# One sample of a residual matmul gathered by GpSimd, without the rows of eight partitions

## The chip, the cores and the metric

The kernel runs on one core of a Trainium2 chip. The metric is the time of one execution on the device in microseconds (us), the median of several runs. The engines of the core are TensorE (PE, matrix products), VectorE (DVE), ScalarE (ACT), GpSimd (POOL) and SyncE (SP). Sixteen DMA engines move data between the large memory (HBM) and the on-chip memory (SBUF, 128 partitions); transfers are issued on queues that belong to an engine.

## The reference

```
x: (128, 128, 1024) f32      # samples b, channels c, times t
subjects: (128,) int32       # one of 8 per sample
weights: (8, 128, 128) f32   # c x d per subject

w = weights[subjects]
out = x + einsum('bct,bcd->bdt', x, w)
```

For each of the 128 samples a 128x128 matrix is chosen by the sample's subject; it is multiplied with the sample (128x1024), and the sample itself is added. 67 MB are read and 67 MB written.

## The kernel before

The samples go in 32 tiles (index `i`) of four samples each, a sample in the tile being `q` from 0 to 3. A tile is worked in two halves of two samples; the halves, here called pairs, have the running number `j` from 0 to 63. Tile `i` lies in buffer `i % 12` of `xs`, with the channels on the 128 partitions, so twelve tiles (24 MB) can be on the chip at once. The order of the work is written out by hand, with semaphores between the engines; no scheduler moves it.

Loads (line 121). ACT issues one transfer of 512 KB for each sample, in order. The source is cut so that four consecutive rows (`ROWS`), 16 KB, are one piece, and the four rows land in four neighbouring partitions. From tile 12 on, ACT first waits until the store of the tile that had the buffer before has landed (line 167). Each buffer has two semaphores `s_pair`, one for each half; every transfer adds 16 (`DMA`) to its half's.

Weights. All eight matrices lie in `w_all` (one transfer of 512 KB, line 161). For every sample GpSimd copies the matrix that the sample's subject names into one of four buffers (line 196); it reads the subjects from `index`, which VectorE prepares at the start (lines 153 to 157). The copy of a pair's first sample waits for the pair's loads and for the add of the pair before (`s_added`), so GpSimd's stream of copies is what releases each pair:

```
nc.gpsimd.wait_ge(s_added, j - P_SLOTS + 1)
copy = nc.gpsimd.tensor_copy(ws[b % W_SLOTS], w_all[:, bass.ds(subject[b % R], 1), :])
copy.wait_op(*loaded(i, q0), "sem-ge")
```

Products and sums. TensorE waits for the pair's copies and makes four products of 128x128 by 128x512 (line 206; a float32 product shows as two matmuls in the profile). VectorE adds the product to the samples, in place, one operation for each pair (line 217).

Stores (line 130). SP stores a whole tile (2 MB) after its second pair, and single halves or samples for the first and the last tile. At the end ACT waits for all stores (line 229).

At the start three matmuls on zeros run on TensorE (line 146). `emptied` and `loaded` compute the values of `s_pair` that mean that a buffer is free or filled.

Of the kernel before, what the change touches and what calls it, by code (L numbers as in the profile page):

```python
# [26 lines left out]
I32 = mybir.dt.int32  # L27
ALU = mybir.AluOpType


G = 2
H = 2
# [3 lines left out]
SLOTS = 12  # L36
# [5 lines left out]
DMA = 16  # L42

IDLE = 3

ROWS = 4
QUEUES = {mybir.EngineType.SP: "qSPDynamicHW", mybir.EngineType.Activation: "qActDynamicHW"}


def transfer(nc, engine, out, in_):  # L50

    later, nc._always_lower_symbolic_ap = nc._always_lower_symbolic_ap, False
    ins, outs = engine.lower_ap_dma(in_), engine.lower_ap_dma(out)
    nc._always_lower_symbolic_ap = later
    return engine.add_instruction(  # L57
        mybir.InstDMACopy(
            name=nc.get_next_instruction_name(),
            engine=engine.engine,  # L60
            ins=ins,
            outs=outs,
            mode="Copy",
            cce_op=ALU.bypass,
            queue=QUEUES[engine.engine],
        )
    )


@with_exitstack  # L70
def kernel(
    ctx: ExitStack,
    tc: tile.TileContext,
    x: bass.AP,
    subjects: bass.AP,
    weights: bass.AP,
    out: bass.AP,
):
    nc = tc.nc
    B, C, T = x.shape  # L80
    S, _, D = weights.shape
    NT = B // (G * H)

    def sbuf(name, *shape, dtype=F32):
        return ctx.enter_context(nc.sbuf_tensor(name, list(shape), dtype)).ap()

    given, near, wrap, index = (
        sbuf(name, 1, B, dtype=I32) for name in ("given", "near", "wrap", "index")
    )
    w_all = sbuf("w_all", C, S, D)  # L90
    ws = [sbuf(f"w{i}", C, 1, D) for i in range(W_SLOTS)]
    zeros = sbuf("zeros", C, N)
    xs = [sbuf(f"x{i}", C, H * G, T) for i in range(SLOTS)]
    ps = [
        ctx.enter_context(nc.psum_tensor(f"ps{i}", [D, G, T], F32)).ap() for i in range(P_SLOTS)
    ]

    s_given = tc.alloc_semaphore("s_given")
    s_wall = tc.alloc_semaphore("s_wall")
    s_index = tc.alloc_semaphore("s_index")  # L100
    s_zeros = tc.alloc_semaphore("s_zeros")
    s_copied = tc.alloc_semaphore("s_copied")
    s_product = tc.alloc_semaphore("s_product")
    s_added = tc.alloc_semaphore("s_added")

    s_pair = [[tc.alloc_semaphore(f"s_pair{i}_{h}") for h in range(H)] for i in range(SLOTS)]


    s_first = tc.alloc_semaphore("s_first")

    def emptied(i, h):

        turns = i // SLOTS
        return (DMA * G + (DMA if h == H - 1 else 0)) * turns

    def loaded(i, q):

        h = q // G
        return s_pair[i % SLOTS][h], emptied(i, h) + DMA * G

    def load(engine, i, q):
        k, h = i % SLOTS, q // G
        transfer(
            nc,
            engine,
            xs[k][:, q, :],
            x[i * H * G + q].rearrange("(a r) t -> a (r t)", r=ROWS),
        ).then_inc(s_pair[k][h], DMA)

    def store(i, q0, q1):  # L130
        k, b = i % SLOTS, i * H * G
        transfer(
            nc,
            nc.sync,
            out[b + q0 : b + q1].rearrange("g d t -> d g t"),
            xs[k][:, q0:q1, :].rearrange("d (o g) t -> d o (g t)", g=min(G, q1 - q0)),
        ).then_inc(s_first if i == 0 and q1 == G else s_pair[k][(q1 - 1) // G], DMA)

    with tc.tile_critical():  # L139

        nc.sync.dma_start(given, subjects.rearrange("(o b) -> o b", o=1)).then_inc(s_given, DMA)

        nc.vector.memset(zeros, 0.0).then_inc(s_zeros, 1)  # L143
        nc.tensor.wait_ge(s_zeros, 1)
        for _ in range(IDLE):
            nc.tensor.matmul(  # L146
                ps[P_SLOTS - 1][:, G - 1, :N], zeros[:, :D], zeros, start=True, stop=True
            )

        nc.vector.wait_ge(s_given, DMA)
        nc.vector.tensor_scalar(near, given, -S, S - 1, ALU.max, ALU.min).then_inc(s_index, 1)  # L153
        nc.vector.wait_ge(s_index, 1)
        nc.vector.tensor_scalar(wrap, near, 0, S, ALU.is_lt, ALU.mult).then_inc(s_index, 1)  # L155
        nc.vector.wait_ge(s_index, 2)
        nc.vector.tensor_tensor(index, near, wrap, ALU.add).then_inc(s_index, 1)  # L157
        nc.gpsimd.wait_ge(s_index, 3)


        nc.scalar.dma_start(w_all, weights.rearrange("s c d -> c s d")).then_inc(s_wall, DMA)  # L161
        for i in range(NT):
            k = i % SLOTS
            if i == SLOTS:
                nc.scalar.wait_ge(s_first, DMA)
            if i >= SLOTS:
                nc.scalar.wait_ge(s_pair[k][H - 1], emptied(i, H - 1))
            for q in range(H * G):
                load(nc.scalar, i, q)


        for j in range(NT * H):
            i, q0, q1 = j // H, j % H * G, (j % H + 1) * G
            k = i % SLOTS
            p = ps[j % P_SLOTS]

            ahead = j < P_SLOTS
            if ahead:  # L180
                nc.tensor.wait_ge(*loaded(i, q0))
            for q in range(q0, q1):
                b = i * H * G + q
                if b % R == 0:
                    _, subject = nc.values_load_multi_w_load_instructions(
                        index[0:1, b : b + R],
                        engines=[mybir.EngineType.Pool],
                        min_val=0,
                        max_val=S - 1,
                        skip_runtime_bounds_check_because="the index is clamped on the chip above",  # L190
                    )
                if b == 0:
                    nc.gpsimd.wait_ge(s_wall, DMA)
                if not ahead and q == q0:
                    nc.gpsimd.wait_ge(s_added, j - P_SLOTS + 1)
                copy = nc.gpsimd.tensor_copy(  # L196
                    ws[b % W_SLOTS], w_all[:, bass.ds(subject[b % R], 1), :]
                )
                if not ahead and q == q0:
                    copy.wait_op(*loaded(i, q0), "sem-ge")  # L200
            copy.then_inc(s_copied, 1)

            nc.tensor.wait_ge(s_copied, j + 1)
            for q in range(q0, q1):
                for t in range(0, T, N):
                    mm = nc.tensor.matmul(  # L206
                        p[:, q % G, t : t + N],
                        ws[(i * H * G + q) % W_SLOTS][:, 0, :],
                        xs[k][:, q, t : t + N],
                        start=True,  # L210
                        stop=True,
                    )
            mm.then_inc(s_product, 1)

            mine = xs[k][:, q0:q1, :]
            nc.vector.wait_ge(s_product, j + 1)
            nc.vector.tensor_tensor(  # L217
                mine, p, mine, ALU.add
            ).then_inc(s_added, 1)

            if i == 0 or q1 == H * G or i == NT - 1:
                nc.sync.wait_ge(s_added, j + 1)
                store(i, q0 if i in (0, NT - 1) else 0, q1 - (b == B - 1))

    with tc.tile_critical() as waits:
        for i in range(NT - SLOTS, NT):
            nc.scalar.wait_ge(s_pair[i % SLOTS][H - 1], emptied(i + SLOTS, H - 1))
        nc.scalar.wait_ge(s_pair[(NT - 1) % SLOTS][0], emptied(NT - 1 + SLOTS, 0) + DMA)  # L230
    last = nc.sync.dma_start(out[B - 1], xs[(NT - 1) % SLOTS][:, H * G - 1, :])

    tc.add_manual_dep(
        last.ins,
        waits.name,
        mybir.DependencyInfo(mybir.DependencyClass.NoSync, mybir.DependencyReason.SCHED_ONLY),
        reason="the end of the program waits for it",
    )
# [27 lines left out]
```

## Time and profile before

| | |
|---|---|
| median of 3 runs | 325.92 us (325.64 to 326.22) |
| the profiled execution | 326.15 us, span of its instructions 324.4 us |
| TensorE busy (matmul) | 240.2 us, 74% |
| VectorE busy | 147.9 us, 46% |
| GpSimd busy | 34.3 us, 11% |
| moved by DMA | 134.85 MB, mean 416 GB/s |

The span is cut into 40 slices of 8.1 us. A digit is the busy share in a slice in tenths, 9 being 90% or more. GpSimd's copies are 296 ns each, 128 of them; its idle time before them is 237.2 us, of which 207.2 us ended with the landing of a load.

### The profile page before, as it was taken

How to read it: one execution, taken by the hardware profiler on the slowest of the kernel's cores; microseconds unless marked ns; L12 is line 12 of the kernel's file. 1: busy time of each engine (PE TensorE's matmuls, PEld its weight loads, DVE VectorE, ACT ScalarE, POOL GpSimd, SP SyncE). 2: the span in 40 equal slices, each digit the busy share in tenths (PEclk: the TensorE clock that was granted, in tenths of full speed). 3: DMA queues.
4: the chain of work that ended last, by engine and by line, in shares of the span. 5: the costliest groups of instructions: out<-in, count | busy, mean ns of one | idle time of the engine just before them, and what ended most of it. 6: DMA issues, size and time to landing. Idle time of an engine off the chain costs nothing.

```text
span 324.4 us, 1608 instructions
## 1 busy us (share of the span) xinstructions
PE 240.2 (74%) x518; PEld 94.5 (29%) x518; DVE 147.9 (46%) x68; POOL 34.3 (11%) x132
## 2 busy tenths in 40 slices
PE   7999987888888888888988888888888768000000
PEld 2444432333333333333333333333333323000000
DVE  1475754555555555555555555554554553200000
POOL 1011110111111111111011111111111010000000
PEclk9999999999999999999999999999999999855555
DMA  7999999999999999999999999999999999999995
GB/s 263 402 418 426 426 421 425 425 425 423 428 425 422 427 418 427 427 424 424 428 423 421 423 427 426 419 429 426 423 426 427 417 435 417 425 427 424 429 426 243
DMA packets 16074, 134.85 MB, mean 416 GB/s; under 512 B 2625, under 2 KB 3650, under 8 KB 3906
## 3 DMA queue, kind: packets, MB, share of 16 engines
q10 hardware_dynamic: 7184, 67.64, 49.8%
q1 hardware_dynamic: 8882, 67.11, 49.3%
q8 instruction: 4, 0.07, 0.1%
q14 instruction: 4, 0.03, 0.0%
HBM read 67.63 MB, written 67.11 MB: 415 GB/s over the span
## 4 chain that ended last, share of the span: by engine, by line
PE 41%; DVE 20%; issue 18%; POOL 4%; DMA 2%; POOLq 1%; ACTq 0%; SPq 0%
PE ps L206 41%; DVE x L217 20%; POOL w L196 4%; DMA x<-in_x_dram 2%; POOLq L196 1%; ACTq L57 0%; ACTq L161 0%; ACTq L262 0%; SPq L139 0%
## 5 line engine op out<-in xcount | busy, mean ns | idle before, releaser
L206 PE MATMUL ps<-x,w 128*128 128x512 f32 x512 | 234.7, 604 | 33.6 <-POOL w L196 32.9
L217 DVE TENSOR_TENSOR x<-ps,x 128x2048 f32<-128x2048 f32 x64 | 146.7, 2292 | 128.1 <-PE ps L206 128.1
L206 PEld LDWEIGHTS ps<-x,w 128*128 128x128 f32 x512 | 92.6, 189 | 176.5 <-issue 92.3
L196 POOL COPY w<-w_all 128x128 f32 x128 | 34.1, 296 | 237.2 <-DMA x<-in_x_dram 207.2
L146 PE MATMUL ps<-zeros 128*128 128x512 f32 x6 | 5.5, 1088 | 1.7 <-DVE zeros L143 1.7
L146 PEld LDWEIGHTS ps<-zeros 128*128 128x128 f32 x6 | 1.8, 328 | 3.7 <-issue 2.1
L143 DVE MEMSET zeros<- 128x512 f32 x1 | 0.5, 485 | 1.1 <-SPq L139 1.1
L153 DVE TENSOR_SCALAR near<-given 1x128 int32<-1x128 int32 x1 | 0.2, 216 | 0.6 <-DMA given<-in_itok_B_dram 0.6
L157 DVE CUSTOM_DVE_ANT_0 index<-near,wrap 1x256 uint16<-1x256 uint16 x1 | 0.3, 278 | 0.0
L155 DVE TENSOR_SCALAR wrap<-near 1x128 int32<-1x128 int32 x1 | 0.2, 215 | 0.0
L253 POOL MEMSET const-float32-0.0<- 128x1 f32 x1 | 0.1, 99 | 0.2 <-issue 0.2
L253 POOL MEMSET const-bfloat16-1.0<- 128x1 bf16 x1 | 0.1, 102 | 0.0
L253 POOL MEMSET const-uint8-127<- 128x1 uint8 x1 | 0.1, 102 | 0.0
L253 POOL MEMSET const-float32-1.0<- 128x1 f32 x1 | 0.1, 99 | 0.0
## 6 DMA issues: line engine op xcount, KB each, us to landing
x<-in_x_dram ACTq DMA_DIRECT2D x128, 512.0 KB, 32.2
out_dram<-x SPq DMA_DIRECT2D x30, 2048.0 KB, 46.9
out_dram<-x SPq DMA_DIRECT2D x3, 1024.0 KB, 13.8
out_dram<-x SPq DMA_DIRECT2D x2, 512.0 KB, 21.0
w_all<-in_L_cond_weights_dram ACTq DMA_DIRECT2D x1, 512.0 KB, 4.3
given<-in_itok_B_dram SPq DMA_DIRECT2D x1, 0.5 KB
```

Source lines behind the costliest of these rows:

```text
L143: nc.vector.memset(zeros, 0.0).then_inc(s_zeros, 1)
L146: nc.tensor.matmul(ps[P_SLOTS - 1][:, G - 1, :N], zeros[:, :D], zeros, start=True, stop=True)
L153: nc.vector.tensor_scalar(near, given, -S, S - 1, ALU.max, ALU.min).then_inc(s_index, 1)
L155: nc.vector.tensor_scalar(wrap, near, 0, S, ALU.is_lt, ALU.mult).then_inc(s_index, 1)
L157: nc.vector.tensor_tensor(index, near, wrap, ALU.add).then_inc(s_index, 1)
L196: copy = nc.gpsimd.tensor_copy(ws[b % W_SLOTS], w_all[:, bass.ds(subject[b % R], 1), :])
L206: mm = nc.tensor.matmul(p[:, q % G, t : t + N], ws[(i * H * G + q) % W_SLOTS][:, 0, :], xs[k][:, q, t : t + N], start=True, stop=True,)
L217: nc.vector.tensor_tensor(mine, p, mine, ALU.add).then_inc(s_added, 1)
L253: nc = _bacc.Bacc("TRN2", target_bir_lowering=False, num_devices=1)
```

## The change

One sample, number 3 of tile 11 (the 48th load, sample 47), no longer comes by ACT's load. GpSimd issues one indirect DMA for it, right behind the copies of pair 19: each partition has an index of the row in HBM that belongs to it, and the row is 4 KB. An index beyond the end of `x` means that nothing is moved for that partition; this is set for partitions 16-19 and 48-51. Their eight rows come in two transfers of four rows each on ACT's queue, at the place where the load stood. The gather waits for both (`s_spared`) and for the index (`s_rows`); pair 23's second copy waits for the gather (`s_gathered`). The counts of the buffer's semaphore are lowered by the one transfer that no longer adds to it.

The index is made at the start: GpSimd counts the rows up (iota), and three small VectorE operations add the number of all rows (`B * C`) where the row's number, cut to the bits 0x5C, is 16.

```
+SPARE = (11, 3, 19)
+SPARED = (16, 48)
+SPARED_BITS = 0x5C
...
+    def load_spared(engine, i, q):
+        for p, landed in zip(SPARED, s_spared):
+            transfer(nc, engine, xs[i % SLOTS][p : p + 4, q, :], x[i * H * G + q, p : p + 4, :]).then_inc(
+                landed, DMA
+            )
+
+    def gather(i, q):
+        nc.gpsimd.wait_ge(s_rows, 4)
+        for landed in s_spared:
+            nc.gpsimd.wait_ge(landed, DMA)
+        nc.gpsimd.indirect_dma_start(
+            xs[i % SLOTS][:, q, :],
+            None,
+            x.rearrange("b c t -> (b c) t"),
+            bass.IndirectOffsetOnAxis(ap=rows, axis=0),
+            bounds_check=B * C - 1,
+            oob_is_err=False,
+        ).then_inc(s_gathered, DMA)
...
+        nc.gpsimd.iota(rows, [[0, 1]], base=(SPARE[0] * H * G + SPARE[1]) * C, channel_multiplier=1).then_inc(
+            s_rows, 1
+        )
+        nc.vector.wait_ge(s_rows, 1)
+        nc.vector.tensor_scalar(mark, rows, SPARED_BITS, None, ALU.bitwise_and).then_inc(s_rows, 1)
+        nc.vector.wait_ge(s_rows, 2)
+        nc.vector.tensor_scalar(mark, mark, SPARED[0], B * C, ALU.is_equal, ALU.mult).then_inc(s_rows, 1)
+        nc.vector.wait_ge(s_rows, 3)
+        nc.vector.tensor_tensor(rows, rows, mark, ALU.add).then_inc(s_rows, 1)
...
-                load(nc.scalar, i, q)
+                (load_spared if (i, q) == SPARE[:2] else load)(nc.scalar, i, q)
...
+                if (i, q) == SPARE[:2]:
+                    nc.gpsimd.wait_ge(s_gathered, DMA)
...
             copy.then_inc(s_copied, 1)
+            if j == SPARE[2]:
+                gather(*SPARE[:2])
```

## The prediction

> **What bounds the kernel now.** I read the two rows of slices first, then the DMA queues, then who waits for whom, and at last the end of the span cut into short stretches.
>
> ```profile
> DVE  1475754555555555555555555554554553200000
> POOL 1011110111111111111011111111111010000000
> DMA  7999999999999999999999999999999999999995
> GB/s 263 402 418 426 426 421 425 425 425 423 428 425 422 427 418 427 427 424 424 428 423 421 423 427 426 419 429 426 423 426 427 417 435 417 425 427 424 429 426 243
> ...
> q10 hardware_dynamic: 7184, 67.64, 49.8%
> q1 hardware_dynamic: 8882, 67.11, 49.3%
> q8 instruction: 4, 0.07, 0.1%
> ...
> x<-in_x_dram ACTq DMA_DIRECT2D x128, 512.0 KB, 32.2
> out_dram<-x SPq DMA_DIRECT2D x30, 2048.0 KB, 46.9
> ```
>
> The 16 DMA engines are full from the second slice to the last but one, at 417 to 435 GB/s. The load queue (q10) and the store queue (q1) share them, 49.8 and 49.3%. No other engine is near that. A store waits 46.9 us from issue to landing, so the stores stand in a long queue; a load waits 32.2 us. So work on the compute engines is late or early without cost as long as neither queue runs dry, and the time is what the slowest DMA engine has to carry.
>
> The next rows are GpSimd's copies in order of time, from the one of pair j = 19 (a pair is two samples) to that of j = 23.
>
> ```profile
> 82.04 0.53 POOL L196 COPY w<-w_all 128x128 f32 x2 [3.46 <-DMA x<-in_x_dram]
> 86.35 0.53 POOL L196 COPY w<-w_all 128x128 f32 x2 [3.77 <-DMA x<-in_x_dram]
> ...
> 98.99 0.53 POOL L196 COPY w<-w_all 128x128 f32 x2 [3.78 <-DMA x<-in_x_dram]
> ```
>
> Each copy has waited for its own pair of samples: the compute runs right behind the loads, one pair in (98.99 - 82.04) / 4 = 4.24 us. Sample 47, the one that the change treats, lands just before 98.99.
>
> Last, the end of the span in short stretches; the last two columns are the mean busy share of the 16 DMA engines and GB/s.
>
> ```profile
> 319.00:320.00 1.00, 0.00 (x0) 0.00 (x0) 0.00 (x0) 0.00 (x0) 0.50 1.02 418
> 320.00:320.40 0.40, 0.00 (x0) 0.00 (x0) 0.00 (x0) 0.00 (x0) 0.50 0.85 348
> 320.40:320.80 0.40, 0.00 (x0) 0.00 (x0) 0.00 (x0) 0.00 (x0) 0.50 0.68 277
> 320.80:321.20 0.40, 0.00 (x0) 0.00 (x0) 0.00 (x0) 0.00 (x0) 0.50 0.38 154
> 321.20:321.60 0.40, 0.00 (x0) 0.00 (x0) 0.00 (x0) 0.00 (x0) 0.50 0.32 133
> 321.60:322.00 0.40, 0.00 (x0) 0.00 (x0) 0.00 (x0) 0.00 (x0) 0.50 0.20 82
> 322.00:322.40 0.40, 0.00 (x0) 0.00 (x0) 0.00 (x0) 0.00 (x0) 0.50 0.10 41
> 322.40:322.90 0.50, 0.00 (x0) 0.00 (x0) 0.00 (x0) 0.00 (x0) 0.50 0.06 25
> 322.90:324.30 1.40, 0.00 (x0) 0.00 (x0) 0.00 (x0) 0.00 (x0) 0.50 0.00 0
> ```
>
> The engines do not end together. 0.06 of 16 engines is one engine: from 322.4 to 322.9 a single one still works, and the share of 0.10 in the stretch before says that the second ended at about 322.25. The trace's records have the last engine's final packet end at 322.95. So the last engine leads the second by 0.7 us and the mean engine by some 1.7, and the program waits for it. It is the only place where a transfer of this size can change the time. The late engines are probably those that carried a 16 KB packet of q8 (program code): four such packets took 0.97 to 1.10 us each in the trace's records, against 0.616 us for a 16 KB packet of a load.
>
> **The base.** The profiled execution took 326.15 us: a span of 324.4 and 1.75 around it. The median shown is 325.92, 0.23 less; I take differences from the profile and apply them to 325.92.
>
> **Part 1, sample 47 without eight partitions.** The load that is dropped is 32 packets of 16 KB (four rows of 4 KB each), two for each engine: 2 x 0.616 = 1.23 us of every engine. The gather brings the sample back in rows of 4 KB, except 16-19 and 48-51: these are just two of the 32 packets, which is what one engine carried. If they are one engine's two, that engine is rid of 1.23 us. The Trainium skill, page "DMA: Bandwidth & Descriptors", section "The descriptor swizzle", puts partitions 16-19 and 48-51 on the same DMA engine; no view of this profile names an engine. What is cut would then be more than the lead of 0.7, so the gain would be the lead and no more.
>
> **Part 2, the gather's own cost on the other 15 engines.** No row of before has a gather. Nearest below: the 4 KB packets of the last stores took 0.159 us each, so eight rows are 1.27 us instead of 1.23, +0.04. Farthest above: the 512-byte pieces of w_all, 512 KB that its 16 engines moved from 2.04 to about 4.8 us, 2.7 us each, so up to +1.5 if a gathered row went in small pieces. A gain below the first is excluded, since the bytes are the same. I take +0.04, because the rows have the size of the store's packets, and keep +1.5.
>
> **Part 3, the eight spared rows.** Two transfers of four rows in place of one load on ACT: one more issue, at 0.48 us (the shortest of the load issues) to 4.3 (the longest); ACT's loads land 32 us after their issue, so this is covered by their queue. On the DMA engines eight rows of 0.159 us. Spread over eight engines this is 0.16 each, over four 0.32, on one 1.27. The one tiny transfer of before (the index list) shows that a small transfer does not use all engines: it is one packet. I take 0.32 on four engines. The same page, section "Why a DMA increments its semaphore by 16 and not by 1", has a transfer of four partitions on four engines, the lowest-numbered; by that the sum would be the same 0.32.
>
> **Part 4, the stall on GpSimd.** The gather stands behind copy 19 and waits for the spared rows. They are last in tile 11's loads: behind sample 46, some 2.1 us before 98.99, so about 97. Until then GpSimd stands still, from 82.6 on. Behind it in its stream are the copies of pairs 20 to 23; TensorE, VectorE and the stores wait for those. Issuing the gather takes GpSimd between 0.48 and 4.3 us (the bounds of ACT's load issue). Copy 20 runs at 97.5 to 101.4 instead of 86.35, 11 to 15 us late, and TensorE is idle for about as long; if its clock falls, the first pair runs like the opening matmuls on zeros (1.06 us each, against 0.43 us from start to start later), +3.4 us. So pair 20 is up to 18.5 us late. What hides it is the store queue. Tile 10's store, due at 97.3, would be issued at about 109 to 116. Tile 9's store, issued at 88.7, lands about 51 us later (the median of the stretch from 60 to 120), at 139.8; only then, or from 137.5 on the first engine, does an engine need tile 10's. The margin is 21 us. After the stall a pair takes 3.43 us (the spacing of the adds at 15.03 and 18.47) against 4.24 of the loads, so the delay is made up in 18.5 / 0.81 = 23 pairs at most, while the store queue stays filled. The loads of tile 12 and later wait for stores that landed in the order and time of before. Pair 23 waits for the gather. If that landed as late as a load does, 32 us after its issue, it would be there at 133 at the latest; tile 11's store would be issued at about 140, and is needed when tile 10's ends, about 151. Cost: nothing. Without the queue of stores it would cost the 11 to 18 us.
>
> **Part 5, the index.** One iota on GpSimd (0.10 us, a memset of 128x1, to 0.30, a copy) and three small VectorE operations (0.22 + 0.22 + 0.28 = 0.7 us by their neighbours) are done before 5.4 us, when the first copy gets its weights, and VectorE is idle until 11.6. Even some us more would only move the first stores, while the loads fill the engines. Cost: nothing.
>
> **Sum.** If the relieved engine is the last: the end moves to the second, -0.70; the gather +0.04; -0.66. If the second is one of the four that take spared rows (about one chance in four), -0.34. I take -0.6: 325.3. That the cut fits the last engine is a choice and not a reading, since no view numbers the engines.
>
> **The rivals.**
> (a) Another engine is last, or the kept-out rows still burden theirs, so the last engine gets the gather's +0.04, 325.9 to 326.0. For it: nothing in the trace ties partitions 16-19 to the lone engine. Against it: if lateness follows from program code, it is the same engine in each run, and one engine's weight is the one thing that this change alters. The page's table in "Rules for kernel authors" says that spreading transfers over the three issuing engines brings no bandwidth. By that the time would be 325.9 as well; that total is not what part 1 is about.
> (b) Slower: the last engine is one of those that take spared rows, or the gather goes in small pieces. The first costs 0.04 + 0.32 = 0.36 (326.3), with all eight rows on it 0.04 + 1.27 = 1.3 (327.2); the second makes the second engine end 1.5 later, so 1.5 - 0.7 = +0.8 (326.7). It decides from 0.65 up: four rows on the last engine, or 1.4 us more for the gather. For it: a transfer of few rows sits on few engines. Against it: the 4 KB packets of the stores run at the rate of the big ones.
> (c) The stall is not hidden: the store queue would have to run dry, which needs pair 20 to be 40 us late (115 + 25 = 140). Nothing points there; then some us more, 328 to 335.
>
> **How the numbers follow.** The forecast 0.45, (a) 0.27, (b) 0.20, (c) 0.03, and 0.05 for more than the lead (the order of the engines' ends may differ without the profile; up to 1.2 us, 324.7). About 0.2%, 0.65 us, is what a measurement of this kernel can tell from no change. The forecast's -0.66 lies on that bound, so I give nearly 6 in 10 of it to faster: 0.27 + 0.05 = 0.32. Of (b) most is over the bound, with (c) 0.19 slower. The rest, 0.49, is within. The forecast's own range is 325.0 to 325.6; to hold 8 in 10 it takes in (a) and most of (b): 324.9 to 326.7.
>
> **What would show it.** Right: in the last stretches the share falls to zero at about 322.3, with the first lone stretch gone; a third hardware or software queue of about 0.49 MB; GpSimd silent from 82.6 to about 98 with the DMA row at 9 throughout; adds 3.4 us apart after it until about 190. Wrong: the lone engine still there at 322.9 or later (a); a longer tail, or a gather queue whose share is well over 0.4% of the engines (b); a dent in the DMA row after 137 (c).

## The result and the profile after

The changed kernel takes 327.14 us (326.78 to 327.42, six runs); the kernel before took 325.84 beside it. The ratio is 1.0035, with a 95% interval from 1.0025 to 1.0045: slower by 1.3 us, where the forecast was 325.3 and the range ended at 326.7. The profiled execution took 327.42 us, with a span of 325.6.

The page of the changed kernel, first the rows of slices, then the DMA queues and the row of the gather:

```profile
PE   6999987888606999999999898888889598000000
DMA  7999999999999999999999999999999999999996
GB/s 260 411 406 423 430 415 419 429 419 421 425 429 420 422 420 420 429 414 423 428 421 420 426 424 416 425 424 424 423 420 422 429 421 421 429 424 429 425 429 263
...
q10 hardware_dynamic: 7152, 67.15, 49.5%
q1 hardware_dynamic: 8882, 67.11, 49.4%
q0 software_dynamic: 144, 0.49, 0.4%
...
L154 POOL DMA_INDIRECT x<-in_x_dram,rows x1 | 1.2, 1168 | 15.6 <-issue 15.6
...
x<-in_x_dram,rows POOLq DMA_INDIRECT x1, 12.6
```

The stall is there (TensorE's slice of 0), and the DMA row stays at 9 through it. The gather has the forecast's 0.49 MB and 0.4% of the engines: in the records 120 packets of 4 KB and 24 of 4 bytes. (The run with all rows, below, has 128 and 16; so each kept-out row still leaves a packet of 4 bytes.) GpSimd's instructions in order of time show the stall and how it is made up:

```profile
82.71 0.53 POOL L240 COPY w<-w_all 128x128 f32 x2 [3.50 <-DMA x<-in_x_dram]
98.80 1.17 POOL L154 DMA_INDIRECT x<-in_x_dram,rows  x1 [15.56 <-issue]
99.98 0.99 POOL L240 COPY w<-w_all 128x128 f32 x4
109.73 0.53 POOL L240 COPY w<-w_all 128x128 f32 x2 [8.76 <-DVE x L263]
113.17 0.53 POOL L240 COPY w<-w_all 128x128 f32 x2 [2.91 <-DVE x L263]
...
168.10 0.53 POOL L240 COPY w<-w_all 128x128 f32 x2 [2.90 <-DVE x L263]
171.84 0.53 POOL L240 COPY w<-w_all 128x128 f32 x2 [3.21 <-DMA x<-in_x_dram]
```

From 109.73 the copies come 3.43 us apart and wait for VectorE; at 171.84 they wait for loads again. Whether the stall costs anything is tested below.

Then the end of the span, in stretches (the last two columns are the share of the DMA engines and GB/s):

```profile
321.60:322.00 0.40, 0.00 (x0) 0.00 (x0) 0.00 (x0) 0.00 (x0) 0.50 0.78 318
322.00:322.40 0.40, 0.00 (x0) 0.00 (x0) 0.00 (x0) 0.00 (x0) 0.50 0.63 256
322.40:322.90 0.50, 0.00 (x0) 0.00 (x0) 0.00 (x0) 0.00 (x0) 0.50 0.42 172
322.90:323.30 0.40, 0.00 (x0) 0.00 (x0) 0.00 (x0) 0.00 (x0) 0.50 0.43 174
323.30:324.00 0.70, 0.00 (x0) 0.00 (x0) 0.00 (x0) 0.00 (x0) 0.50 0.17 70
324.00:324.60 0.60, 0.00 (x0) 0.00 (x0) 0.00 (x0) 0.00 (x0) 0.50 0.02 7
```

All engines end later: seven of 16 (0.43) still work at 323, where before a single one was left at 322.4. Chained packet by packet, the trace's records give 16 ends; their mean went from 321.1 to 322.7 us. (The 16 increments of the last store's semaphore, 0.4 us behind, went from 321.52 to 323.13.) So it is not one engine that got more; something cost the engines 1.6 us on average.

Where it went is seen when the span is cut by what the queues do: from 40 to 240 us loads and stores alternate, from 280 to 315 only stores are left. Before, then after:

```profile
40.00:240.00 200.00, 174.96 (x380) 68.11 (x379) 108.65 (x48) 25.09 (x94) 1.00 1.01 425
280.00:315.00 35.00, 0.00 (x0) 0.00 (x0) 0.00 (x0) 0.00 (x0) 0.51 1.01 426
```

```profile
40.00:240.00 200.00, 171.75 (x377) 70.16 (x377) 107.72 (x48) 26.04 (x95) 0.96 1.01 422
280.00:315.00 35.00, 0.00 (x0) 0.00 (x0) 0.00 (x0) 0.00 (x0) 0.51 1.01 427
```

Engines fully busy in both, but 422 GB/s instead of 425 while the queues alternate, and no loss with stores alone. In the records of that stretch a store's 8 KB packet took 314.8 ns on average instead of 312.1, a load's 16 KB packet 619.35 instead of 616.5. The loss shows from about 28 us on, 9 us behind the first store and 70 us ahead of the gather. Each engine moves 268 of the first and 190 of the second in 200 us: 268 x 2.7 + 190 x 2.84 ns = 1.26 us. As an estimate that is 1.5 us over the 242 us (28 to 270) in which the loss shows.

The compute engines have no part in it. During the stall none of them does anything, and the loss is the same: from 90 to 98.8 us the packets took 314.7 and 620.3 ns.

```profile
90.00:98.80 8.80, 0.00 (x0) 0.00 (x0) 0.00 (x0) 0.00 (x0) 0.50 1.00 419
```

### The profile page after: what moved, and what is told of

Read it like the earlier page. It is cut to its first block, busy times and chain, and to the rows that moved or that the text cites. A ratio compares the mean times of both kernels' runs of the same rounds, so it can differ in the third digit from the quotient of the medians.

```text
span 325.6 us, 1618 instructions
## 1 busy us (share of the span) xinstructions
PE 239.2 (73%) x518; PEld 97.9 (30%) x518; DVE 148.2 (46%) x71; POOL 35.3 (11%) x134
## 4 chain that ended last, share of the span: by engine, by line
PE 37%; ACTq 20%; DMA 9%; DVE 8%; issue 8%; POOL 2%; POOLq 0%; SPq 0%
PE ps L252 37%; ACTq L63 20%; DMA x<-in_x_dram 9%; DVE x L263 8%; POOL w L240 2%; POOLq L240 0%; ACTq L203 0%; POOL x L154 0%; POOLq L153 0%; POOLq L154 0%; ACTq L308 0%; SPq L172 0%
## 5 line engine op out<-in xcount | busy, mean ns | idle before, releaser
L252 PEld LDWEIGHTS ps<-x,w 128*128 128x128 f32 x512 | 96.0, 193 | 173.8 <-issue 96.2
L154 POOL DMA_INDIRECT x<-in_x_dram,rows x1 | 1.2, 1168 | 15.6 <-issue 15.6
## 6 DMA issues: line engine op xcount, KB each, us to landing
x<-in_x_dram,rows POOLq DMA_INDIRECT x1, 12.6
```

Source lines behind the costliest of these rows:

```text
L154: nc.gpsimd.indirect_dma_start(xs[i % SLOTS][:, q, :], None, x.rearrange("b c t -> (b c) t"), bass.IndirectOffsetOnAxis(ap=rows, axis=0), ...
L252: mm = nc.tensor.matmul(p[:, q % G, t : t + N], ws[(i * H * G + q) % W_SLOTS][:, 0, :], xs[k][:, q, t : t + N], start=True, stop=True,)
```

## The experiments

What of the change works before the gather is issued? Two things were left. Theory A: the two index tiles (`rows`, `mark`) are allocated ahead of the weights and the samples. They take 32 bytes each in every partition, so all that lies behind them moves: the sample buffers begin at byte 26816 of a partition instead of 26752 (by the order and sizes of the tiles; no trace shows an address). Theory Q: the program now has a third queue, GpSimd's, and the engines lose time on it. The kernels of one group ran on one chip beside the kernel before (medians 325.97, 325.89 and 325.96 in the three groups). The packet times below are means of the records from 40 to 240 us.

**The shift alone.** The kernel before with an unused tile:

```
+    pad = sbuf("pad", C, 16)          # 64 bytes a partition
     w_all = sbuf("w_all", C, S, D)
```

> The kernel before with nothing but an unused tile of 64 bytes for each partition ahead of w_all, so that the sample buffers begin at byte 26816 of a partition instead of 26752, as in the changed kernel. In the changed kernel the packets of both queues take longer from the first store on, long before the gather: 622.5 against 619.3 ns for 16 KB of a load and 313.3 against 311.5 ns for 8 KB of a store, some 1.6 us for each DMA engine. Theory A (the shift of the buffers by 64 bytes does it): 325.84 + 1.6, about 327.4, with packets of 622 and 313 ns. Theory Q (the third queue, GpSimd's, does it): 325.8 as before, 619 and 311 ns.

Measured: 327.52 us, ratio 1.0049 (1.0037 to 1.0062); packets of 314.7 and 619.5 ns (over the whole run 313.2 and 621.4, the 313 and 622 of theory A). No gather, no third queue, and the whole loss. Its two stretches:

```profile
40.00:240.00 200.00, 173.89 (x377) 67.60 (x376) 107.81 (x48) 24.88 (x94) 1.00 1.01 422
280.00:315.00 35.00, 0.00 (x0) 0.00 (x0) 0.00 (x0) 0.00 (x0) 0.50 1.01 426
```

422 and 426 GB/s, as in the changed kernel. Theory Q falls.

**The change without the shift.** The changed kernel with `rows` and `mark` allocated behind the sample buffers:

```
-    rows = sbuf("rows", C, 1, dtype=I32)
-    mark = sbuf("mark", C, 1, dtype=I32)
     w_all = sbuf("w_all", C, S, D)
...
     xs = [sbuf(f"x{i}", C, H * G, T) for i in range(SLOTS)]
+    rows = sbuf("rows", C, 1, dtype=I32)
+    mark = sbuf("mark", C, 1, dtype=I32)
```

> The changed kernel with its two small tiles (rows, mark) allocated behind the sample buffers, which begin at byte 26752 again. Theory A: packets of 619 and 311 ns again, 327.14 - 1.6 = 325.5, and if the relieved engine was the last one, 325.2. Theory Q: 327.1, as the changed kernel.

Measured: 325.68 us, ratio 0.9993 (0.9984 to 1.0001); packets of 312.0 and 617.2 ns. The loss is gone with the shift. Of the two times of theory A the 325.5 came nearer than the 325.2: beside its own kernel before (325.97) the gain is 0.3 us, and the interval still holds 1. The end of its span:

```profile
321.60:322.00 0.40, 0.00 (x0) 0.00 (x0) 0.00 (x0) 0.00 (x0) 0.50 0.43 174
322.00:322.40 0.40, 0.00 (x0) 0.00 (x0) 0.00 (x0) 0.00 (x0) 0.50 0.03 10
322.40:322.90 0.50, 0.00 (x0) 0.00 (x0) 0.00 (x0) 0.00 (x0) 0.50 0.00 0
```

Seven engines (0.43 of 16) work nearly to 322; in the records the last ends at 322.30 and the second at 322.12, against 322.95 and 322.25 before. The lone engine is gone, as forecast.

**Which tile's address.** The kernel before with the 64 bytes right ahead of the samples, so that the weights stay where they were:

```
+    pad = sbuf("pad", C, 16)
     xs = [sbuf(f"x{i}", C, H * G, T) for i in range(SLOTS)]
```

> The kernel before with 64 unused bytes right ahead of the sample buffers: these begin at byte 26816 as in the changed kernel, the weights and the zeros stay where they were. If the samples' address is what matters: 327.5, as with the shift of all. If that of the weights does (GpSimd copies, TensorE loads): 325.9.

Measured: 327.46 us, ratio 1.0047 (1.0033 to 1.006), packets of 314.6 and 620.25 ns. It is the samples' address.

**Which addresses.** The kernel before with unused tiles of 32, 128, 192, 256 and 384 bytes ahead of `w_all`:

```
+    pad = sbuf("pad", C, 32)          # 128 bytes; 8, 48, 64 and 96 for the others
     w_all = sbuf("w_all", C, S, D)
```

> The kernel before with an unused tile of 128 bytes ahead of w_all: the sample buffers begin at byte 26880, a multiple of 256 (26752 is 128 above one, 26816 is 192 above one). Theory A in the form that only multiples of 128 matter: 325.8. In the form that a multiple of 256 is better still: below 325.8, down to some 324.7 if the 1.1 us that the packets of before took above 616 and 311 ns goes as well. In the form that any shift hurts: 327.4. Theory Q: 325.8.

> The kernel before with 384 unused bytes ahead of w_all: the sample buffers begin at byte 27136, a multiple of 256 and of 512 (26880 is one of 256 alone). If 256 is what matters: 325.15, as with 128 bytes. If a multiple of 512 is better still: below 324.9.

> The kernel before with 256 unused bytes ahead of w_all: byte 27008, again 128 above a multiple of 256. If the address within 256 bytes is all that counts: 325.9, as before, 312 ns for 8 KB of a store beside loads. If it is how far the buffers are moved: anything else.

> The kernel before with 32 unused bytes ahead of w_all: the sample buffers begin at byte 26784, 160 above a multiple of 256. If the packets are longest where the address is odd in 64 and shorter the rounder it is (0: 310.7 ns for 8 KB of a store beside loads, 128: 312, 64 more: 314.7): no shorter than with 64 bytes, 327.5 or more. If only distance from a multiple of 128 counts: between, 326.5 to 327.

> The kernel before with 192 unused bytes ahead of w_all: byte 26944, 64 above a multiple of 256. If the address within 128 bytes sets the loss: 327.5, as with 64 bytes (192 above one). If a distance of 64 is better than one of 192: 325.2 to 326.

Measured, by the distance of the sample buffers above a multiple of 256 bytes:

| bytes above a multiple of 256 | unused bytes | time, us | ratio (95%) | 8 KB of a store, ns | 16 KB of a load, ns |
|---|---|---|---|---|---|
| 0 | 128 | 325.15 | 0.9972 (0.9961 to 0.9982) | 310.65 | 616.2 |
| 0 | 384 | 325.10 | 0.9975 (0.9965 to 0.9985) | 310.7 | 616.05 |
| 64 | 192 | 327.40 | 1.0041 (1.0029 to 1.0054) | 314.4 | 619.6 |
| 128 | none | 325.84 to 325.97 | 1 | 312.1 | 616.5 |
| 128 | 256 | 325.88 | 0.9993 (0.9984 to 1.0003) | 312.0 | 616.9 |
| 160 | 32 | 326.90 | 1.0021 (1.0011 to 1.003) | 313.4 | 618.3 |
| 192 | 64 | 327.52 | 1.0049 (1.0037 to 1.0062) | 314.7 | 619.5 |

With a shift of 256 bytes the time is that of before: how far the buffers move is nothing, the address within 256 bytes is what counts. A multiple of 256 is best, and one of 512 no better. The kernel before was itself not at the best address. Of the readings on record, "a multiple of 256 is better still" (128 bytes), "256 is what matters" (384), "the address within 256 bytes" (256) and "the address within 128 bytes" (192) held. Of the two for the 32-byte run the first missed and the second held: an address of 160 is 32 from a multiple of 128 and costs less than 64 and 192, which are 64 from one. So, at the addresses tried, a store's packet beside loads grows from 312 over 313.4 to 314.4 or 314.7 ns with the distance from the nearest multiple of 128, and a multiple of 256 is 1.4 ns better than the other multiples of 128. The kernel with 128 unused bytes, in the two stretches:

```profile
40.00:240.00 200.00, 175.61 (x382) 68.29 (x381) 109.24 (x48) 24.88 (x94) 1.00 1.01 426
280.00:315.00 35.00, 0.00 (x0) 0.00 (x0) 0.00 (x0) 0.00 (x0) 0.50 1.01 426
```

Now the mixed stretch moves as much as the stores alone. With stores alone the packets take 310.9 ns at every one of these addresses. With loads alone the address does count: from 6 to 16 us, ahead of the first store, the median load packet took 612 ns in the three profiles with the samples at a multiple of 256 and 636 to 640 ns in all eleven others. There 128 is no better than 64 or 192, so this part tells a multiple of 256 from the kernel before, but not the kernel before from the changed one.

The Trainium skill, page "DMA: Bandwidth & Descriptors", section "How a descriptor splits into AXI transactions", says that a transaction must start at a multiple of 256 bytes, so that a descriptor which does not start at one also fetches bytes that it does not use. That agrees with 256 as the period and with the best address. It does not give the order: by that rule a start 128 bytes above wastes more than one 64 above, and here 64 costs 3.7 ns a store packet and 128 only 1.4; and stores alone lose nothing at any address. So the address is shown to be the cause, and by which mechanism it acts on the transfers is open.

**Is it the engine of 16-19 and 48-51?** The run with the index last, but with other partitions kept out, and with none (all 128 rows gathered, no spared rows, no wait for them):

```
-SPARED = (16, 48)
+SPARED = (0, 32)                      # the first; () for the second
```

> As the run with the index tiles last, but partitions 0-3 and 32-35 are kept out of the gather instead of 16-19 and 48-51. If keeping out 16-19 and 48-51 takes 1.2 us from the last DMA engine, this one is slower than that run by 0.3 to 0.7 us, and its last engine ends alone again. If it does nothing for the end, both are equal within 0.2 us.

> As the run with the index tiles last (325.68), but no partition is kept out: the gather brings all 128 rows, no spared rows come by the loads' queue, and the gather waits for nothing. If keeping out 16-19 and 48-51 was what made the lone last engine go: it is back, one engine ending 0.5 us or more after the others, at 325.9 to 326.2. If not: 325.7 and no lone engine.

Measured: 325.90 us, ratio 0.9999 (0.999 to 1.0007), and 326.14 us, ratio 1.0002 (0.9994 to 1.0011). The ends of their spans, first with 0-3 and 32-35 kept out, then with all rows gathered:

```profile
322.00:322.40 0.40, 0.00 (x0) 0.00 (x0) 0.00 (x0) 0.00 (x0) 0.50 0.07 31
322.40:322.90 0.50, 0.00 (x0) 0.00 (x0) 0.00 (x0) 0.00 (x0) 0.50 0.04 16
```

```profile
322.00:322.40 0.40, 0.00 (x0) 0.00 (x0) 0.00 (x0) 0.00 (x0) 0.50 0.08 31
322.40:322.90 0.50, 0.00 (x0) 0.00 (x0) 0.00 (x0) 0.00 (x0) 0.50 0.06 25
```

The lone engine is back in both; the records have it end 0.9 and 1.0 us after the second. With 16-19 and 48-51 kept out (this run and that of the next paragraph) the last leads by 0.15 to 0.2 us only. With the samples at the same address, the unchanged kernel's lead was 0.7 us, and 0.4 with 256 unused bytes; it varies, but stays larger.

The records also show that the eight kept-out rows are one engine's. In the run with the index last the first nine of the gather's 24 packets of 4 bytes come one behind the other from 103.09 to 108.38 us, at steps of 0.32, 0.63 or 0.93 us: a store's packet of 311 ns between them, a load's of 616, or both. That is one engine that goes on with the other two queues and has no row to bring; the other 15 packets follow from 109.85 us on. All five runs with rows kept out show these nine, the run with 0-3 and 32-35 too; with all rows the 16 packets of 4 bytes all stand in the last microsecond. The Trainium skill, page "DMA: Bandwidth & Descriptors", section "The descriptor swizzle", puts the four partitions from 16 and the four from 48 on one engine; the trace agrees.

So, with the samples at this address, the engine that ends last is that of 16-19 and 48-51 as far as one profile of each run can show; why it is that one stays open. What the relief is worth in time is small: the 23 executions with them kept out (the run with the index last and the run of the next paragraph) have a mean of 325.73 us, the 24 of these two 326.08, so 0.34 us, with a standard error of 0.08. By its time alone the run with 0-3 and 32-35 fits neither of its two readings (0.22 us slower, where 0.3 to 0.7 or no more than 0.2 was named). The single intervals overlap; the four medians (325.68, 325.69 against 325.90, 326.14) stand in order.

**Does the stall cost anything?** The run with the index last, with the gather behind pair 22:

```
-SPARE = (11, 3, 19)
+SPARE = (11, 3, 22)
```

> As the run with the index tiles last (325.68), but the gather is issued behind the copies of pair 22 instead of 19, so that GpSimd waits some 2 us for the spared rows instead of 15.6. If the queue of stores hides the stall: the same within 0.2 us, and the granted clock of TensorE nearer to that of the kernel before. If the stall costs something: faster by 0.3 us or more.

Measured: 325.69 us, ratio 0.9993 (0.9984 to 1.0002), beside 325.68 with the stall, at a mean granted clock of 0.912 against 0.904 (0.933 before). GpSimd in order of time:

```profile
93.96 0.53 POOL L240 COPY w<-w_all 128x128 f32 x2 [3.58 <-DMA x<-in_x_dram]
97.77 1.17 POOL L154 DMA_INDIRECT x<-in_x_dram,rows  x1 [3.28 <-issue]
98.95 0.30 POOL L240 COPY w<-w_all 128x128 f32 x1
110.17 0.29 POOL L240 COPY w<-w_all 128x128 f32 x1 [10.92 <-DMA x<-in_x_dram,rows]
```

The wait of 15.6 us went to 3.3, but now the second copy of pair 23 waits 10.9 us for the gather itself. So this run moved a stall more than it removed one. The two runs of the paragraph before tell more. Neither has the relief of the last engine, and their gathers waited 16.3 us (0-3 and 32-35 kept out) and 0.5 us (all rows):

```profile
97.90 1.17 POOL L154 DMA_INDIRECT x<-in_x_dram,rows  x1 [16.29 <-issue]
```

```profile
82.15 1.17 POOL L154 DMA_INDIRECT x<-in_x_dram,rows  x1 [0.48 <-issue]
```

The run with the stall took 325.90 us (ratio 0.9999 to its own kernel before), the one without 326.14 (1.0002). The stall costs nothing that these runs can tell.

**The change at the best address.** The changed kernel with 64 unused bytes more, so that the samples begin at a multiple of 256:

```
     mark = sbuf("mark", C, 1, dtype=I32)
+    pad = sbuf("pad", C, 16)
     w_all = sbuf("w_all", C, S, D)
```

> The changed kernel with 64 more unused bytes behind its index tiles, so that the sample buffers begin at byte 26880, a multiple of 256. Theory A in its new form (the address of the buffers within 256 bytes sets the length of the packets; the change itself, without the shift, gains 0 to 0.6 us): the step from the 64-byte to the 128-byte shift of the kernel before was 327.52 - 325.15 = 2.4 us, so 327.1 - 2.4 = 324.7, the best of all. If the change has a cost of its own beside the address: 325.2 or more.

Measured: 325.20 us, ratio 0.9977 (0.9967 to 0.9986). That is 1.9 us less than the changed kernel for an unused 64 bytes, but no better than the kernel before with its samples at such an address (325.10 and 325.15): the change gains nothing there. The 324.7 expected was missed, and 325.20 falls on the other reading, a cost of the change beside the address. In the records of the kernel before the last engine ends 0.3 us after the second with 128 unused bytes, at 321.87, and 0.1 us with 384, so little is left to take; here the last three end within 0.04 us, at 322.35, with the mean end 0.3 to 0.4 us later. Whether that is a cost of the change, one profile each cannot tell: two profiles of the kernel before at one address (64 unused bytes) differ by 0.3 as well. No kernel of the record beats the one before with 128 or 384 unused bytes: 0.25 to 0.28% faster than before.

## Why the prediction was wrong

It forecast 325.3 and the kernel took 327.14; neither the sign nor the range held.

**The step that failed** is part 5, "the index ... Cost: nothing", and with it the sum, which costed only the packets of sample 47. I priced the index by its instructions, which did hide: iota 0.12 us, the three operations 0.13 to 0.16 us each. I did not ask where its tiles lie. They moved every sample buffer by 64 bytes, and the other 127 loads and all stores took 0.5 to 0.9% longer per packet while the queues alternate: some 1.5 us on every engine by the packets, 1.6 by the mean of their ends, which nothing covers, since the DMA engines are the bound. Without the shift the kernel takes 325.68.

**Parts 1 and 2 held in kind; the size did not.** By the runs with and without the relief the relieved engine was the last, and the last end moved from 322.95 to 322.30 in the records of the run without the shift, beside the -0.66 of the sum. That this is so close is luck: the unchanged kernel with 256 unused bytes ended at 322.83. In the medians the gain is half, 325.68 against 325.97, -0.3 (ratio interval 0.9984 to 1.0001), where -0.6 was taken. That the two pieces are one engine's was called a choice and not a reading; it proved right. The gathered rows took 161 ns for each 4 KB, against the forecast's 159 and far from the +1.5 us of small pieces.

**Part 3**: the records show the eight spared rows as 4 KB packets of 159 ns. The loads' queue has eight packets of 4 bytes for the two transfers together, where one whole load has 16; that fits the four engines that were taken. Which engines cannot be read, but their cost did not make a receiving engine end alone.

**Part 4 held.** GpSimd waited 15.56 us and TensorE's granted clock fell to 0.5, pair 20's copy began at 99.98 (13.6 us late), its add came at 107.28 instead of 90.68 (16.6 us late, within the 11 to 18.5), the pairs then followed 3.43 us apart, the DMA row stayed at 9, and the delay was made up by 171.84, earlier than the 190 that I gave as a limit. The run with the gather elsewhere had the same time. One reading in this part is wrong: 1.06 us is how long an opening matmul took, and their weight loads began 0.85 us apart; the +3.4 us follows from 0.85 against 0.43, and measured was 3.0.

**The rivals.** (a), another engine last, is refuted by the two runs with other or no partitions kept out and the order of the small packets. (b) had the right sign for a wrong reason; neither of its two mechanisms showed. (c) did not occur. None of the rivals was one of addresses, so the 0.19 that I gave to slower was for other causes. The sign that would have shown it early was named for (b) only: a longer tail.

## What to carry to other kernels

A new tile, however small, moves all that is allocated after it; where transfers are the bound, put small tiles behind the large buffers and look at the buffers' address within 256 bytes before a change is judged (here 64 bytes cost 1.5 us and 128 gained 0.8, both more than the change was worth). A loss that is spread over every packet, from a time before the changed operation runs, is not that operation's doing: compare the packets by stretch first.

## What the runs showed of the hardware

I had not expected the address of a buffer on the chip to matter to the DMA at all. With stores alone it does not (310.9 ns a packet at every address). With loads alone a packet took 612 ns at a multiple of 256 bytes and 636 to 640 elsewhere. While both queues run it cost bandwidth, 422 against 425 and 426 GB/s, though not from the first: from 20 to 24 us the changed kernel's packets took 309 and 611 ns, as at the best address. Why is open.

Nor had I expected a gather of 120 rows to take 12.6 us from issue to landing beside two full queues, when its packets take 161 ns each and an engine has eight of them. In the records they spread from 103.2 to 111 us, since each engine goes on with the other two queues between them.
